# The order of matmuls between attention blocks: projection by halves, product D behind A, the 1x1 convolution behind three taps

## The chip, the core and the metric

The kernel runs on one core of a Trainium2 chip. The time is the device time of one execution, in microseconds (us); several runs are made and their median is compared. A core has a matmul engine (TensorE, PE in the profile, with its weight loads as PEld), a vector engine (VectorE, DVE), an activation engine (ScalarE, ACT), GpSimd (POOL), and SyncE (SP), which issues transfers. Each has its own instruction stream; they meet at semaphores. Matmul results go to PSUM, an accumulator of eight banks of 512 fp32 columns by 128 partitions.

## The reference

Input is x of 8 images, 64 channels, 64 by 64 pixels, fp32. Two layers follow each other.

```
q, k, v = 1x1 projections of x                 # 64 to 64 channels
q, k    = q - mean(q), k - mean(k)             # mean over the pixels
out     = softmax(q^T k / 8) v  +  softmax(mean(q)^T k) v
x2      = x + out
s       = bn(conv1x1(sign(x2))) + bn(conv3x3(sign(x2))) + bn(conv5x5(sign(x2)))
gate    = sigmoid(grouped 16x16 product of mean(s) + gb), channels permuted
result  = s * gate + x2
```

The convolution weights are signs (of the weights less their mean) times a scale for each output channel. So the convolutions are products of numbers like -1, 0 and 1 and can be done in bf16 without loss; the attention stays in fp32.

## The kernel before

Two images lie together on the 128 partitions (64 channels each), which makes four pairs. A pair has 8 query blocks (`NQ`) of 512 pixels, and a block has 32 key tiles (`NK`) of 128 pixels: 32 blocks in all, g = 0 to 31.

**Main loop** (`attend`, line 904). For each key tile j: `scores` (line 461, four matmuls on 64x64 quarters of the array, into one of two score buffers of two banks, pool `ps_s`), an exponential on ACT (line 472, tile `e`, four buffers), then for the tile before it `weighted` (line 480, accumulated in `acc`, the only buffer of pool `ps_a`) and `summed` (line 495, on DVE, which adds up the e tiles). Every instruction is put down in this order by hand (`manual_schedule`); `plan(g)` says what else goes behind which key tile.

**Between blocks.** Behind the first key tile's scores of block g and the last `weighted` of block g-1 come, in this order: `weighted_out` (line 502, ACT copies `acc` to SBUF), in some blocks a small matmul (the gate, the mean scores of the next pair, or the unary part), then `mix_rows` (line 824), then `sums` (line 511, the softmax denominators, tile `su`). `mix_rows` does two things at once on the array: the projection of the queries of block g+1, and the convolutions of block g-3. This happens with both parts in 28 passages between blocks, and once more, without the projection, at the last block. Only the first blocks have a projection alone, and near the end another routine (`mix`) takes over.

**What mix_rows computes.** The projection `q` is split by pixels in two tiles: pq of half 0 has 128 columns, pq of half 1 has 384 (`split_queries`, line 446). Both are fp32[...]. The 5x5 convolution is done for pairs of output rows: `S` (10 products of 256 columns) goes to both rows of a pair, `D` (5 products) to both with opposite signs, `A` and `B` (10 each) to one row each (`row_product`, line 660). The 1x1 is one product of 512 columns and the 3x3 nine (`conv_tap`, line 725). "Half" h means the half of the array's rows (partitions 0 to 63 or 64 to 127) that feeds a product; b, the image, is the half of its columns. Half 0 does q of half 0, S, 1x1 and 3x3; half 1 does q of half 1, D, A and B; each for b = 0 and 1.

**What sets their order.** Each of the four sequences (b, h) gives each of its products a length in units (0.5 for 256 columns of bf16, 1.0 for 512; q is 1.0 in half 0 and 3.0 in half 1) and so a nominal start; all are sorted by it (line 845), and the second key of the sort decides among those with equal starts.

**Where results go.** PSUM tiles of tag "m" (pool `ps_m`, two buffers of one bank) are taken in turn by pq of half 0, pq of half 1, then zD and z1 at their first product, and then by su. z3 uses a bank of the `acc` buffer. S, A and B (tile z5) use a score buffer: S one bank, A and B the halves of the other. The reads are: `split_queries_out` (line 453, DVE, twice), which frees the pq buffers; for D two ACT instructions that start the sum tile `sb` (line 682); adds to `sb` on DVE (line 678) for 1, for S (twice), for A and for B; a copy of z3 by ACT (line 698); and the last add on DVE (line 703). A result whose name is in the test inside the loop ("D1") is read out as soon as its products are in the stream; the others follow behind the loop, in the order of the string there ("3SAB").

Of the kernel before, what the change touches and what calls it, by code (L numbers as in the profile page):

```python
# [44 lines left out]
def conv_seq_kernel(ctx, tc, x, wq, wk, wv, vecs, w1, w3, w5, wtap, gw, out):  # L45
# [16 lines left out]
    def m_tile(name):  # L62
        return ps_m.tile([P, QB], F32, tag="m", name=name)
# [760 lines left out]
    def mix_rows(q, c):  # L824


        seqs = {}
        for b in range(2):
            half0, half1 = [], []
            if q is not None:  # L830
                half0.append(("q", 0, 1.0))
                half1.append(("q", 0, 3.0))
            if c is not None:
                sums = [("S", i, 0.5) for i in range(10)]
                half0 += sums + [("1", 0, 1.0)] + [("3", i, 1.0) for i in range(9)]
                half1 += [("D", i, 0.5) for i in range(5)]
                half1 += [(n, i, 0.5) for n in "AB" for i in range(10)]
            seqs[b, 0], seqs[b, 1] = half0, half1
        order = []
        for (b, h), seq in seqs.items():  # L840
            at = 0.0
            for t in seq:
                order.append((at, b != h, b, h, t))
                at += t[2]
        order.sort(key=lambda o: o[0:2])
        if c is not None:
            p, (r0, _, y, qb) = c
            z, name = {}, f"{p.name}_{qb}"
        if q is not None:
            q[0].query_tiles(q[1])  # L850
        left = {}
        for o in order:
            left[o[4][0]] = left.get(o[4][0], 0) + 1
        for _, _, b, h, (n, i, _) in order:
            if n == "q":
                q[0].split_queries(q[1], b, h)
            else:
                if n not in z:
                    if n in "1D":
                        z[n] = m_tile(f"z{n}_{name}")  # L860
                        if n == "D":
                            z[n] = z[n][:, 0 : QB // 2]
                    elif n == "3":
                        z[n] = acc_banks(f"z3_{name}")[0]
                    elif n in "SAB":
                        t = score_banks(f"z5_{name}")
                        z["S"] = t[0][:, 0 : QB // 2]
                        z["A"], z["B"] = t[1][:, 0 : QB // 2], t[1][:, QB // 2 :]
                if n in "13":
                    p.conv_tap((r0, ROWS, y, qb), {0: [z.get("1")], 1: [z.get("3")]}, b, 0, int(n) // 2, i, i == 0, i == 8 or n == "1")  # L870
                else:
                    p.row_product(z, b, (n, i), r0)
            left[n] -= 1
            if left[n] == 0:
                if n == "q":
                    q[0].split_queries_out(q[1])
                elif n in "D1":
                    p.row_out(qb, z, n)
        if c is not None:
            for n in "3SAB":  # L880
                p.row_out(qb, z, n)
            p.row_end(qb)

# [20 lines left out]
    def attend(pairs):  # L904
# [9 lines left out]
        def plan(g):  # L914
# [26 lines left out]
            def both():  # L941
                q = block(g + 1) if g + 1 < n_blocks else None
                if g == 0:
                    mix(q, None)
                else:
                    mix_rows(q, rows(g - 3) if g >= 3 else None)
# [270 lines left out]
```

## Time and profile before

| | |
|---|---|
| time, median of 3 runs | 1993.19 us (1992.76 to 1994.49) |
| span of the profiled execution | 1993.0 us |
| granted TensorE clock, mean | 0.995 of full speed |
| from one passage's su to the next | 59.87 us, or 60.90 in blocks that also compute the next pair's values |
| key-tile iteration | 1.72 us |
| scores, exponential, weighted: one instruction | 591 ns, 1024 ns, 589 ns |
| 64x256 bf16 product, record | 270 ns |
| L682 (ACT, D), L678 (DVE, 1x1 add), L703 | 1.02 us for two, 0.75, 0.75 us |

In the profile a line such as L660 is a line of the code; "out<-in" names the tiles; the number after x is how many instructions the row joins. The records of the four quarters overlap, so a busy matmul engine may have quarters without work. In the list of waits the first name is who waited and the second who let it go. In the timeline the first column is the start and the second the duration, both in us.

### The profile page before, as it was taken

What the parts mean: (1) busy time and instruction counts of PE and PEld (TensorE: products, weight loads), DVE (VectorE), ACT (ScalarE), POOL (GpSimd) and SP (SyncE); (2) the same over time, 40 slices, a digit from 0 to 9 for tenths busy, and PEclk for the clock granted to TensorE, in tenths of its full rate; (3) what the DMA queues carried; (4) which work ended last, traced back from release to release, by engine and by line L of the source; (5) the groups of instructions that cost most, each with busy time, mean ns of one, the idle gap of its engine ahead of it and who ended that gap; (6) DMA issues with size and microseconds to landing.
All of it is one profiled execution on the core that took longest, in us unless ns stands there. A gap on an engine that the chain in (4) does not pass through costs nothing.

```text
span 1993.0 us, 48278 instructions
## 1 busy us (share of the span) xinstructions
PE 1959.4 (98%) x20946; PEld 777.4 (39%) x20946; DVE 1565.2 (79%) x1739; ACT 1251.8 (63%) x1474; POOL 5.9 (0%) x26
## 2 busy tenths in 40 slices
PE   9999999999999999999999999999999999999997
PEld 4333334343433333343433333333343333333334
DVE  6878877778777798777777778887777778877876
ACT  5666666666666666666666666666666666666663
POOL 0000000000000000000000000000000000000000
PEclk9999999999999999999999999999999999999998
DMA  3010000000001010000001001000000001100001
GB/s 98 9 49 17 14 17 10 15 13 14 17 9 59 17 51 17 15 11 13 15 14 49 19 27 43 14 17 14 13 11 16 14 17 36 32 14 17 17 12 45
DMA packets 43212, 45.84 MB, mean 23 GB/s; under 512 B 15968, under 2 KB 34608, under 8 KB 42864
## 3 DMA queue, kind: packets, MB, share of 16 engines
q1 hardware_dynamic: 42240, 41.49, 7.7%
q8 instruction: 166, 2.72, 0.6%
q10 hardware_dynamic: 720, 1.18, 0.2%
q14 instruction: 54, 0.44, 0.1%
q0 software_dynamic: 32, 0.01, 0.0%
HBM read 14.89 MB, written 8.39 MB: 12 GB/s over the span
## 4 chain that ended last, share of the span: by engine, by line
PE 94%; DVE 4%; ACT 1%; issue 1%; DMA 0%; DVEq 0%; SPq 0%; ACTq 0%
PE ps L461 43%; PE acc L480 42%; PE z L660 2%; DVE es L495 2%; PE z L725 2%; PE pq L446 1%; PE su L511 1%; PE zD L660 1%; PE pv L303 1%; DVE q L453 1%; ACT e L472 0%; DMA x<-in_x 0%; PE warm L149 0%; PE pre L1060 0%; PE po L350 0%
## 5 line engine op out<-in xcount | busy, mean ns | idle before, releaser
L472 ACT ACTIVATE e<-ps 128x1024 f32<-128x1024 f32 x1024 | 1048.9, 1024 | 625.4 <-PE ps L461 589.3
L495 DVE TENSOR_TENSOR es<-es,e 128x1024 f32<-128x1024 f32 x960 | 1170.9, 1220 | 283.4 <-ACT e L472 261.9
L461 PE MATMUL ps<-q,x 64*64 64x512 f32 x8192 | 1067.7, 591 | 0.9 <-DVE kb L159 0.9
L480 PE MATMUL acc<-e,v 64*64 64x512 f32 x8192 | 1063.9, 589 | 0.6 <-ACT e L472 0.3
L480 PEld LDWEIGHTS acc<-e,v 64*64 64x64 f32 x8192 | 310.0, 131 | 570.3 <-ACT e L472 302.6
L461 PEld LDWEIGHTS ps<-q,x 64*64 64x64 f32 x8192 | 307.8, 133 | 543.7 <-issue 286.6
L660 PE MATMUL z<-ec,wc 64*64 64x256 bf16 x580 | 79.4, 272 | 0.0
L678 DVE SCALAR_TENSOR_TENSOR sb<-z,scale,sb 128x256 f32<-128x256 f32 (+1 forms) x87 | 46.9, 566 | 41.1 <-ACT sb L682 41.1
L725 PE MATMUL z<-s,wt 64*64 64x512 bf16 (+2 forms) x694 | 78.6, 367 | 0.5 <-ACT s L591 0.3
L660 PEld LDWEIGHTS <-wc 64*64 64x64 bf16 x1450 | 66.5, 106 | 20.8 <-issue 20.7
L725 PEld LDWEIGHTS <-wt 64*64 64x64 bf16 x860 | 67.5, 107 | 4.6 <-issue 3.0
L524 DVE RECIPROCAL rc<-su 128x128 f32<-128x128 f32 x62 | 58.9, 950 | 0.0
L660 PE MATMUL z<-rs,wc 64*64 64x256 bf16 x435 | 57.8, 270 | 0.0
L682 ACT ACTIVATE sb<-zD,shift,half 128x256 f32<-128x256 f32 x58 | 29.6, 562 | 34.7 <-PE zD L660 34.7
L591 ACT ACTIVATE s<-x,vec 128x512 bf16<-128x512 f32 (+2 forms) x66 | 46.1, 702 | 5.2 <-DVE x L559 5.2
L453 DVE TENSOR_SCALAR q<-pq,mx 128x128 f32<-128x128 f32 (+1 forms) x60 | 26.2, 479 | 29.1 <-PE pq L446 29.1
L493 DVE TENSOR_TENSOR es<-e,e 128x1024 f32<-128x1024 f32 x32 | 39.2, 1224 | 11.1 <-ACT e L472 11.1
L698 ACT COPY r_z<-z 128x512 f32<-128x512 f32 x29 | 17.0, 586 | 37.8 <-PE z L725 37.8
L660 PE MATMUL z<-ec,wt 64*64 64x256 bf16 x290 | 37.9, 274 | 0.0
L660 PE MATMUL z<-rs,wt 64*64 64x256 bf16 x290 | 37.9, 274 | 0.0
L678 DVE SCALAR_TENSOR_TENSOR sb<-z,half,sb 128x256 f32<-128x256 f32 x58 | 25.4, 479 | 12.9 <-PE z L660 12.8
L660 PEld LDWEIGHTS <-wt 64*64 64x64 bf16 x580 | 33.8, 107 | 0.1
(146 smaller groups left out, 686.8 us busy)
## 6 DMA issues: line engine op xcount, KB each, us to landing
r<-rc SPq DMA_DIRECT2D x248, 32.0 KB, 1.9
x<-in_x SPq DMA_DIRECT2D x15, 512.0 KB, 6.1
out<-sb SPq DMA_DIRECT2D x28, 256.0 KB, 2.1
ec<-rs SPq DMA_DIRECT2D x29, 153.0 KB, 2.4
xc<-in_x SPq DMA_DIRECT2D x30, 96.0 KB, 2.5
s<-s SPq DMA_DIRECT2D x31, 66.0 KB, 2.0
y<-y SPq DMA_DIRECT2D x30, 64.0 KB, 2.0
w_tap<-in_wtap SPq DMA_DIRECT2D x2, 560.0 KB, 10.0
```

What stands on the lines that cost most here:

```text
L453: nc.vector.tensor_scalar(q[:, c], self.pq[h][:, 0 : c.stop - c.start], self.mx, None, ALU.subtract)
L461: nc.tensor.matmul(ps[img[h], b, :], self.x[img[b], bass.ds(j * P + h * H, H)], self.q[qb][img[b], :], start=True, stop=neg is None,)
L472: nc.scalar.activation(e, ps, AF.Exp, scale=1.0 / 8.0)
L480: nc.tensor.matmul(self.acc[qb][img[b], h, :], self.v[img[h], j, img[b]], e[img[h], b, :], start=(j == 0), stop=(j == NK - 1),)
L493: nc.vector.tensor_tensor(self.es[qb], self.first, e, ALU.add)
L495: nc.vector.tensor_tensor(self.es[qb], self.es[qb], e, ALU.add)
L524: nc.vector.reciprocal(self.rc[:, c], self.sums_p[:, c])
L591: nc.scalar.activation(sy[n][0][:, rows, pad : pad + HH], self.x2[qb][:, r0 * HH : r1 * HH].rearrange("p (h w) -> p h w", w=HH), AF.Sign, ...
L660: nc.tensor.matmul(z[name][img[b], :].rearrange("p (h w) -> p h w", w=HH), taps[k][img[h], c * C : c * C + C], rows, start=(i == 0), stop= ...
L678: nc.vector.scalar_tensor_tensor(out, data, scale, out, ALU.mult, ALU.add, **kw)
L682: nc.scalar.activation(sv[:, :, t, :], z["D"].rearrange("p (j w) -> p j w", w=HH), AF.Identity, bias=shift, scale=half5[:, t : t + 1],)
L725: nc.tensor.matmul(z[n][h][img[b], 0 : nr * HH].rearrange("p (h w) -> p h w", w=HH), wt[img[h], FIRST[n] + i, :], data, start=first, stop= ...
```

## The change

The order of work inside `mix_rows` is rearranged. (1) Among products with equal nominal start, those of half 0 come first for both images, where before the diagonal quarters came first; so the two short projection matmuls stand ahead of the two long ones. (2) In half 1, D comes behind A, not ahead of it. (3) In half 0, the 1x1 comes behind three taps of the 3x3. (4) The 1x1 result is no longer read within the loop but behind it, and its add stands behind those of S, A and B. The purpose is that products that need a buffer which the projection holds come later than those that don't, and that the add which frees the score buffer comes ahead of those which free less. The products, their number and sizes stay as they are.

```diff
             if c is not None:
                 sums = [("S", i, 0.5) for i in range(10)]
-                half0 += sums + [("1", 0, 1.0)] + [("3", i, 1.0) for i in range(9)]
-                half1 += [("D", i, 0.5) for i in range(5)]
-                half1 += [(n, i, 0.5) for n in "AB" for i in range(10)]
+                taps3 = [("3", i, 1.0) for i in range(9)]
+                half0 += sums + taps3[0:3] + [("1", 0, 1.0)] + taps3[3:]
+                for n, k in (("A", 10), ("D", 5), ("B", 10)):
+                    half1 += [(n, i, 0.5) for i in range(k)]
             seqs[b, 0], seqs[b, 1] = half0, half1
         order = []
         for (b, h), seq in seqs.items():
             at = 0.0
             for t in seq:
-                order.append((at, b != h, b, h, t))
+                order.append((at, h, b, h, t))
                 at += t[2]
         order.sort(key=lambda o: o[0:2])
...
-                elif n in "D1":
+                elif n == "D":
                     p.row_out(qb, z, n)
         if c is not None:
-            for n in "3SAB":
+            for n in "3SAB1":
                 p.row_out(qb, z, n)
             p.row_end(qb)
```

## The prediction

> **What bounds the kernel now.** I read the page first (busy shares and the chain that ended last), then the list of waits, then the timeline of one passage between two blocks. TensorE is the bound everywhere:
>
> ```profile
> PE 1959.4 (98%) x20946; PEld 777.4 (39%) x20946; DVE 1565.2 (79%) x1739; ACT 1251.8 (63%) x1474; POOL 5.9 (0%) x26
> PE 94%; DVE 4%; ACT 1%; issue 1%; DMA 0%; DVEq 0%; SPq 0%; ACTq 0%
> ```
>
> The first line is busy time, the second the chain by engine. The 4% of VectorE in the chain says that the matmul engine is at times held by it, and a busy 98% doesn't say that all four 64x64 quarters of the array work. The list of waits names the places the change can touch (us in total, times, longest):
>
> ```profile
> DVE sb L678 <- ACT sb L682: 41.1, 29, 2.3
> ACT sb L682 <- PE zD L660: 34.7, 28, 2.5
> DVE q L453 <- PE pq L446: 29.1, 30, 1.0
> PE zD L660 <- DVE q L453: 12.5, 28, 0.5
> PEld ps L461 <- DVE sb L678: 7.7, 28, 0.3
> ```
>
> Only the last two are waits of the matmul engine, the others are idle time of engines with room. The one of zD comes 28 times, once in each passage that has a projection and a convolution. A passage between 316 and 323 us:
>
> ```profile
> 316.46 0.27 PE L446 MATMUL pq<-x,mm 64*64 64x128 f32 x1
> 316.68 0.27 PE L660 MATMUL z<-rs,wc 64*64 64x256 bf16 x1
> 316.77 1.01 ACT L502 COPY o<-acc 128x1024 f32<-128x1024 f32 x1
> 316.79 0.48 PE L446 MATMUL pq<-xc,mm 64*64 64x384 f32 x1
> 317.12 0.27 PE L660 MATMUL z<-rs,wc 64*64 64x256 bf16 x1
> 317.41 0.88 DVE L453 TENSOR_SCALAR q<-pq,mx 128x128 f32<-128x128 f32 x2 [1.00 <-PE pq L446]
> 317.81 0.27 PE L660 MATMUL zD<-rs,wc 64*64 64x256 bf16 x1 [0.42 <-DVE q L453]
> 318.59 1.02 ACT L682 ACTIVATE sb<-zD,shift,half 128x256 f32<-128x256 f32 x2 [0.82 <-PE zD L660]
> 320.77 0.64 PE L511 MATMUL su<-es,ones 128*32 128x256 f32 x8
> 320.81 0.87 DVE L678 SCALAR_TENSOR_TENSOR sb<-z,half,sb 128x256 f32<-128x256 f32 x2 [0.42 <-PE z L660]
> 321.61 0.86 DVE L678 SCALAR_TENSOR_TENSOR sb<-z,scale,sb 128x256 f32<-128x256 f32 x2
> ```
>
> The columns are start, duration, instruction, and in brackets the idle time before it. The passage is from the projection's start (316.46) to the sums of the next block (su, 320.77): 4.31 us. In it, zD needs one of two PSUM buffers (tag "m") that both hold the projection pq. It gets one when the first L453 has read it, and that starts only at 317.41, since the last write of the first pq is the fourth matmul in program order, behind both long ones (second passes at 316.79). The S products stop at 317.12, so nothing streams from about 317.23 (317.12 plus one 0.11 step) to 317.81: 0.58 us, of which the trace counts 0.42, since a matmul's record runs on 0.16 past its stream (0.27 less 0.11).
>
> **What the Trainium skill says.** "TensorE: Matmul & The Clock Gate", Part 3 (The mechanism): matmuls in different tiles of the array overlap, but start and end in strict program order. The overlap agrees: four quarters advance one 64x256 product each per 0.11 us. The strict order does not: the S product at 316.68 starts ahead of the projection's second pass at 316.79, which belongs to an earlier instruction. I follow the trace and keep the page's order as a rival. "TensorEngine Tiling (Array Packing)", Gotcha 1: different row tiles may not use one PSUM bank at the same time. The new order keeps to it (S and A lie in two banks, and D, 1 and 3 have their own), so it costs nothing; no trace shows a collision. "Perfetto Trace Analysis", Optimization Strategy: find the gaps of the most contended engine and what blocks it; that is the zD wait.
>
> **The change part by part.**
>
> *Projection of half 0 first.* The four matmuls are the same, now in the order h0, h0, h1, h1. The first pq is complete after two short ones, at about +0.37 from the start (0.22 of streaming, 0.16 of tail), not +0.95. The first L453 (0.36) can then end by about +0.8, the second (0.5) by +1.5, instead of +1.31 and +1.83. Neighbours in the same row half are no loss: half steps of half 1 already issue two such in a row at 0.11 a step.
>
> *D behind A.* What follows the projection in half 1 is ten A products, which need no "m" buffer but a bank of the score buffer that S already has. zD is first needed at 0.66 (384 columns in two passes: +0.34 plus 0.32) plus ten steps of 0.11, +1.76. Its buffer is free by +0.8, at worst +1.35. The wait of zD goes.
>
> *1x1 behind three taps.* z1 needs the second pq buffer; it now comes at 0.22 + 10 x 0.11 + 3 x 0.22 = +1.98, after its release at +1.5 (at worst +1.87). In its place 3x3 comes first, at 0.22 + 1.10 = +1.32. That needs the accumulator bank, which L502 releases at 317.78, +1.32, plus 0.04 as between L453 and zD: a wait of some 0.04 us takes over. Bounds: 0 and 0.1 (if the restart of the quarters costs as much again).
>
> *Length without stalls.* Half 0 sets it: 0.22 + 0.01 + ten S at 0.11 + ten 512-column taps at 0.22 + 0.09 of tail before su = 3.62. The last convolution of the kernel, with no projection, is a check from the trace: its first z starts at 1899.82, su at 1903.27, 3.45, against my 3.62 - 0.22 = 3.40. With the 0.04: 3.66.
>
> *A new wait of su.* su reuses the buffer of zD, which ACT must have read twice (L682, 1.02). D ends at 0.66 + 15 x 0.11 + 0.04 = +2.35, its record at +2.51; ACT from +2.55 to +3.57; su from +3.61. That is 0.05 ahead of when su would start anyway: just hidden, and behind su on TensorE stands everything. Bounds: nothing, or 0.1 if half 1 lags a step. The S adds wait for the same ACT pair and for the end of the products (+3.7), so they start as before relative to su.
>
> *Adds: S, A, B ahead of 1 and 3.* S, S, A, B still take 1.7 us after su and release the score bank that the third score block (323.11) needs, its weights at 322.68: 0.17 us of room now (322.47 plus 0.04), unchanged. The 1x1 add (0.75, at 319.64 now, in idle time) moves behind them. VectorE is then 0.75 later with the first es add; in the steady loop it idles 0.49 an iteration, so it has caught up after two. In the three blocks that also store (716 to 743 us) it is saturated, but the matmuls keep their 1.72 an iteration there, and it idled 1.7 us earlier in that block. At the two passages after them the mean's matmul waits behind its queue; I allow 1 us in all, between 0 and 2.
>
> *Sum.* 19 regular passages: 4.31 - 3.66 = 0.65, so 12.4. Nine carry a small matmul first (mean, unary or gate; 3 each), whose result blocks the second pq; from there to su is 4.35 (683.83 to 688.18). There half 0 runs ahead, half 1 needs 0.66 + 25 x 0.11 + 0.09 = 3.50, and su waits for ACT until 3.57: 0.78 each, 7.0. Less 1.0: 18.4. 1993.2 - 18.4 = 1974.8, about 1975.
>
> **The rivals.** *Only what the trace counts comes back:* 12.5 us, 1980.7; with strict program order S would start at +0.34 and not +0.22, 28 x 0.12 = 3.4 off the gain, 1978. Together some 1980. For it: the page, and new waits within 0.1 of biting. Against: the S start. *Waits swap places:* 3x3 on L502, su on L682 and the bank release each lose 0.2, and the time stays near 1993. For it: three margins of 0.05 to 0.17. Against: each is a difference of measured times, and not all add. *Slower:* if D ends only with the whole mix, su stands behind 1.02 of ACT plus 0.08; 1.10 - 0.65 = +0.45 a passage, 28 times: 2006. For it: D is later than before, and su has everything behind it. Against: ten B products (1.1 us) follow D in half 1.
>
> **How the numbers follow.** Forecast 0.69, half-way case 0.16, swap 0.06, slower 0.09. One passage (502 to 507 us) runs at a granted clock of 0.66; its coming or going is worth some 2 us, and the new-wait bounds (28 x 0.1 = 2.8) come on top: 1971 below. Above, the half-way case and its spread: 1982. Faster takes the first two, 0.85; same 0.06; slower 0.09.
>
> **What would show it.** zD's wait for L453 gone from the list; 3x3's first tap behind L502 by under 0.1; su behind L682 by under 0.1; the passage near 3.66; L703 0.75 later after su. I am wrong if su names L682 with some tenths, if S starts later than +0.22, or if the score weights slip behind L678.

## The result and the profile after

The changed kernel takes 1974.8 us (median of 4 runs, 1973.93 to 1977.97), the kernel before in the same comparison 1993.84 us (4 runs, 1992.76 to 1994.88). The ratio is 0.9907, with a 95% interval of 0.989 to 0.9925: about 19 us faster. The prediction was 1975.0, between 1971 and 1982.

The page of the profile after shows the same two lines as were shown of before, busy time and the chain that ended last:

```profile
PE 1951.9 (99%) x20946; PEld 776.0 (39%) x20946; DVE 1565.9 (79%) x1739; ACT 1250.8 (63%) x1474; POOL 5.9 (0%) x26
PE 92%; DVE 3%; DMA 3%; ACT 2%; issue 1%; DVEq 0%; SPq 0%; ACTq 0%
```

TensorE has the same 20946 matmuls and is as good as always busy, before and after; the page alone would not tell that anything was gained. The 3% of DMA is nearly all (2.1%) put down to 18 loads of `xc`, the pixels of a later projection, of 2.3 us each. ACT's second read of zD waits for several semaphores, one of them that of such a load, and the load lands about when this read starts. But this read starts 0.46 us after the first read in the kernel after and also in the version "D inside A" below, whose chain has 0% of DMA; so the load holds nothing up. The start of the program varies: the first su lay at 80.89 and 78.71 us in two profiles of the unchanged kernel. So from here on two measures leave the start out: the length of a passage between blocks, from the projection's first matmul to su, and the time from the third su to the last, which holds 27 of the 28 passages with a projection and the last one without. That time is 1704.10 us before and 1686.58 after, 17.5 less of the 19.7 us between the two spans; of the rest, 2.1 lie ahead of the third su.

The list of waits answers the one of before. zD's wait for L453 (12.5 us, 28 times) is no longer in it, and L453 now idles 15.9 us and not 29.1 for the projection. One wait of a TensorE queue is new, the weights of su behind L682:

```profile
ACT sb L682 <- PE zD L660: 49.5, 29, 2.9
DVE q L453 <- PE pq L446: 15.9, 33, 0.7
PEld su L511 <- ACT sb L682: 9.8, 29, 0.4
```

A passage in the timeline of after (start, duration, instruction, idle time before it), the one that stood between 316 and 323 us before:

```profile
313.68 0.27 PE L446 MATMUL pq<-x,mm 64*64 64x128 f32 x1
313.90 0.27 PE L660 MATMUL z<-rs,wc 64*64 64x256 bf16 x1
313.99 1.01 ACT L502 COPY o<-acc 128x1024 f32<-128x1024 f32 x1
314.01 0.48 PE L446 MATMUL pq<-xc,mm 64*64 64x384 f32 x1
314.14 1.05 DVE L453 TENSOR_SCALAR q<-pq,mx 128x128 f32<-128x128 f32 x2 [0.51 <-PE pq L446]
...
315.05 0.40 PE L725 MATMUL z<-s,wt 64*64 64x512 bf16 x2
...
315.53 0.27 PE L660 MATMUL zD<-ec,wc 64*64 64x256 bf16 x1
...
315.92 0.41 PE L725 MATMUL z<-s,wt 64*64 64x512 bf16 x2
315.98 0.27 PE L660 MATMUL zD<-rs,wc 64*64 64x256 bf16 x1
...
316.38 1.02 ACT L682 ACTIVATE sb<-zD,shift,half 128x256 f32<-128x256 f32 x2 [1.38 <-PE zD L660]
...
317.45 0.16 PEld L511 LDWEIGHTS su<-es,ones 128*32 128x32 f32 x8 [0.36 <-ACT sb L682]
317.45 0.64 PE L511 MATMUL su<-es,ones 128*32 128x256 f32 x8
317.60 0.88 DVE L678 SCALAR_TENSOR_TENSOR sb<-z,half,sb 128x256 f32<-128x256 f32 x2 [2.40 <-PE z L725]
318.39 1.65 DVE L678 SCALAR_TENSOR_TENSOR sb<-z,scale,sb 128x256 f32<-128x256 f32 x3
```

Each fp32 matmul of the projection stands in the trace as two records, its two passes (240 records for 120 matmuls): 313.68 is a first pass, 314.01 a second one. The passage is 317.45 less 313.68, 3.77 us, where it was 4.31. L453 starts 0.46 after the passage's start and not 0.95, zD starts without a wait, the first tap of the 3x3 comes 0.05 after L502 has ended (313.99 + 1.01 = 315.00). At its end su waits: L682 ends at 317.40 and su starts at 317.45.

The whole gain, by passages, in us each:

| | before | after | times | gain |
|---|---|---|---|---|
| plain passage | 4.31 | 3.77 | 19 | 10.3 |
| with the mean scores first | 4.73 | 4.03 | 3 | 2.1 |
| with the unary part first | 6.54 | 4.23 | 1 | 0.7, and 1.6 of clock |
| the same, at full clock | 4.93 | 4.23 | 2 | 1.4 |
| with the gate first | 5.45 | 4.75 | 3 | 2.1 |
| the last, without a projection (from its first S to su) | 3.45 | 3.66 | 1 | -0.2 |
| the first two, with a projection alone | 1.97, 1.91 | 1.38, 1.31 | 2 | 1.2 |

The sum is 19.2, for 19.0 between the medians. In the first two passages su needs the buffer that L453's first read gives back, and before it waited 0.52 us for it in each; now that read is done in time. The clock entry is the passage from 502 us on, which ran at a low granted clock before. Its block took 64.44 us where its two like took 62.83; after, all three take 62.13. That is 0.70 less for the two and 2.3 less for the one, 1.6 beyond the 0.70. The stretches of before, then of after, around this passage (stretch; length, busy time of PE, PEld, DVE, ACT, POOL; granted clock; DMA):

```profile
500.00:502.00 2.00, 1.79 (x22) 1.25 (x23) 0.39 (x2) 1.14 (x5) 0.00 (x0) 1.00 0.00 0
502.00:504.00 2.00, 1.56 (x30) 1.56 (x33) 0.87 (x2) 0.25 (x1) 0.00 (x0) 0.59 0.17 49
504.00:506.00 2.00, 2.00 (x37) 2.00 (x33) 0.75 (x1) 0.77 (x2) 0.00 (x0) 0.55 0.09 25
```

```profile
496.00:498.00 2.00, 1.85 (x44) 1.59 (x47) 1.14 (x4) 0.72 (x5) 0.00 (x0) 1.00 0.00 0
498.00:500.00 2.00, 2.00 (x60) 2.00 (x54) 0.20 (x1) 0.79 (x2) 0.00 (x0) 1.00 0.26 73
```

PE is busy in both; it is the column ahead of the DMA's, the clock, that falls to 0.59 and 0.55 in one and stays at 1.00 in the other. Taken over 502.4 to 505.8 us alone it is 0.50. The profile of the kernel after has such a stretch too, at another place: 0.51 from 79.1 to 82.5 us. It cost about as much: from the first su to the second there are 59.19 us, against 57.49 in the version "D inside A", which has the same two first passages and the full clock there.

### The profile page after: what moved, and what is told of

It is laid out like the page before. It is cut to its first block, busy times and chain, and to the rows that moved or that the text cites. A ratio compares the mean times of both kernels' runs of the same rounds, so it can differ in the third digit from the quotient of the medians.

```text
span 1973.3 us, 48307 instructions
## 1 busy us (share of the span) xinstructions
PE 1951.9 (99%) x20946; PEld 776.0 (39%) x20946; DVE 1565.9 (79%) x1739; ACT 1250.8 (63%) x1474; POOL 5.9 (0%) x26
## 4 chain that ended last, share of the span: by engine, by line
PE 92%; DVE 3%; DMA 3%; ACT 2%; issue 1%; DVEq 0%; SPq 0%; ACTq 0%
PE ps L461 43%; PE acc L480 43%; DVE es L495 2%; DMA xc<-in_x 2%; PE z L660 1%; PE su L511 1%; PE z L725 1%; PE pq L446 1%; PE pv L303 1%; ACT e L472 1%; ACT sb L682 1%; DMA x<-in_x 0%; ACT o L502 0%; PE warm L149 0%; PE po L350 0%
## 5 line engine op out<-in xcount | busy, mean ns | idle before, releaser
L660 PEld LDWEIGHTS <-wc 64*64 64x64 bf16 x1450 | 78.8, 105 | 1.1 <-issue 0.6
L660 PE MATMUL z<-ec,wc 64*64 64x256 bf16 x580 | 73.7, 270 | 0.0
L682 ACT ACTIVATE sb<-zD,shift,half 128x256 f32<-128x256 f32 x58 | 29.6, 560 | 49.5 <-PE zD L660 49.5
L725 PEld LDWEIGHTS <-wt 64*64 64x64 bf16 x860 | 46.1, 105 | 5.8 <-issue 3.3
L453 DVE TENSOR_SCALAR q<-pq,mx 128x128 f32<-128x128 f32 (+1 forms) x60 | 29.0, 484 | 17.4 <-PE pq L446 15.9
L502 ACT COPY o<-acc 128x1024 f32<-128x1024 f32 (+2 forms) x33 | 32.3, 982 | 1.2 <-PE acc L480 1.2
L446 PE MATMUL pq<-xc,mm 64*64 64x128 f32 (+1 forms) x120 | 29.3, 385 | 2.7 <-ACT gt L764 2.0
```

What stands on the lines that cost most here:

```text
L446: nc.tensor.matmul(self.pq[h][img[b], 0:w], mm[img[h], img[h]], data, start=True, stop=True)
L660: nc.tensor.matmul(z[name][img[b], :].rearrange("p (h w) -> p h w", w=HH), taps[k][img[h], c * C : c * C + C], rows, start=(i == 0), stop= ...
L682: nc.scalar.activation(sv[:, :, t, :], z["D"].rearrange("p (j w) -> p j w", w=HH), AF.Identity, bias=shift, scale=half5[:, t : t + 1],)
L725: nc.tensor.matmul(z[n][h][img[b], 0 : nr * HH].rearrange("p (h w) -> p h w", w=HH), wt[img[h], FIRST[n] + i, :], data, start=first, stop= ...
```

## The experiments

The theory from the prediction: what counts is when the first pq is complete and who asks for its buffer; each part of the change then has a place in that chain. The rivals: the sort alone would do it; D's place alone would do it; the 1x1's place matters, or doesn't; the order of the adds is for nothing; and a late D costs more than it brings. Each ratio is to the kernel before on the same chip in the same comparison (1994.65 us in the first four, 1993.02 in the next four, 1992.53 in the last two). Most of the intervals overlap with that of the change (0.989 to 0.9925); where they do, what is said below of a difference rests on the traces. "Special" passages are those with mean scores, unary part or gate first.

| kernel | median, us | ratio, 95% interval | plain passage | third su to last |
|---|---|---|---|---|
| sort alone | 1977.78 | 0.9922 (0.9904 to 0.994) | 3.86 | 1690.33 |
| change with the old sort | 1974.53 | 0.9896 (0.988 to 0.9913) | 3.74 | 1686.18 |
| change with the 1x1 add ahead of S | 1984.65 | 0.9946 (0.993 to 0.9963) | 3.77 | 1696.25 |
| old sort, 1x1 ahead of the 3x3 | 1976.72 | 0.9906 (0.989 to 0.9923) | 3.75 | 1687.19 |
| D inside A | 1973.02 | 0.9904 (0.9888 to 0.9921) | 3.66 | 1684.04 |
| D last | 2007.21 | 1.0075 (1.0058 to 1.0092) | 4.89 | 1718.13 |
| D inside A, 1x1 add in the loop | 1971.82 | 0.9895 (0.9879 to 0.9912) | 3.66 | 1684.06 |
| before once more | 1994.3 | 1.0006 (0.9997 to 1.0015) | 4.31 | 1704.16 |
| half 1 first behind the projection | 1971.81 | 0.9892 (0.9875 to 0.9908) | 3.66 | 1684.71 |
| 1x1 first, D behind eight A | 1971.75 | 0.9889 (0.9873 to 0.9906) | 3.61 | 1683.23 |

**The sort alone**, the kernel before with only the projection's order changed:

```diff
-                order.append((at, b != h, b, h, t))
+                order.append((at, h, b, h, t))
```

> The kernel before with the sort key alone changed (half 0 first among equal starts). My theory (zD waits because the first pq counts as written only when the fourth matmul in program order is done): the first read of pq ends near +0.82 us from the start of the projection, zD wants its buffer at +0.66 and waits about 0.2 instead of 0.58, z1 at +1.32 then waits for the second read, ending near +1.5. Passage about 3.85 us against 4.31, nine passages with a small matmul 0.6 shorter; time about 1980. Rival (the move of D behind A is what brings the gain, the sort nothing): within 4 us of before, 1990 or more.

Measured: 1977.78, a plain passage of 3.86, the special ones 0.44 shorter than before (0.6 were expected). zD starts 0.86 after the passage's start:

```profile
311.76 0.27 PE L446 MATMUL pq<-x,mm 64*64 64x128 f32 x1
...
312.62 0.27 PE L660 MATMUL zD<-ec,wc 64*64 64x256 bf16 x1
...
313.32 0.40 PE L725 MATMUL z<-y,wt 64*64 64x512 bf16 x2
```

The long projection matmuls have streamed at +0.66, so zD still stands some 0.2 behind L453's first read, but S goes on meanwhile and the list counts no wait. This one line takes 13.8 us (1704.10 less 1690.33) of the 17.5; 1.6 of either are the clock's. What it also leaves is that z1, first of the 512-column products, waits for the second pq buffer (L453 ends its second read at 313.27, z1 starts at 313.32).

**The change with the old sort**, so without the line above:

```diff
-                order.append((at, h, b, h, t))
+                order.append((at, b != h, b, h, t))
```

> The changed kernel with the old sort key: D behind A, 1x1 behind three taps, 1x1 add last, but the projection in its old order. My theory: zD is then needed at +1.76 and its buffer is free at +1.35 also with the old projection, z1 at +1.98 against +1.87, so nothing waits: as the changed kernel, 1975 within 2 us. Rival (the order of the projection is needed as well): z1 or zD still wait some tenths, 1980 or more.

Measured: 1974.53 and 3.74, a shade shorter than the whole change. The two parts are two ways to the same half microsecond: the sort lets the first buffer go earlier, D behind A asks for it later. With D behind A the sort is not needed in these passages. In the first two, with a projection alone, it is: they take 1.97 and 1.90 here, as before, and 1.38 and 1.31 in every version with the new sort.

**The 1x1 add ahead of S**, all else as in the change:

```diff
-            for n in "3SAB1":
+            for n in "31SAB":
```

> The changed kernel with the 1x1 add ahead of the S, A and B adds. My theory: the add waits for ACT's start of sb, which with D this late ends only as the passage ends, so the score bank comes free 0.75 us later, which eats the 0.17 us of room and costs about 0.6 to 0.7 us in each of 29 passages: about 1994. Rival (the order of the adds lies off the path, VectorE has room): 1975 within 1.5 us.

Measured: 1984.65, 9.7 us in the time from the third su to the last, so 0.35 a passage. It isn't in the passage (3.77) but behind it. The timeline of this experiment:

```profile
317.92 0.75 DVE L678 SCALAR_TENSOR_TENSOR sb<-z,scale,sb 128x512 f32<-128x512 f32 x1 [2.24 <-PE z L725]
317.94 0.64 PE L511 MATMUL su<-es,ones 128*32 128x256 f32 x8
319.57 0.87 DVE L678 SCALAR_TENSOR_TENSOR sb<-z,scale,sb 128x256 f32<-128x256 f32 x2
320.56 0.24 PEld L461 LDWEIGHTS ps<-q,x 64*64 64x64 f32 x8 [0.98 <-PE ps L461]
320.59 1.09 PE L461 MATMUL ps<-q,x 64*64 64x512 f32 x8
```

The add of the 1x1 (0.75) stands ahead of the adds of S, A and B, which free the score bank at 320.44 (319.57 + 0.87), 2.50 after su, and the score block follows at 320.59, 2.65 after su. In the kernel after, the add of B ends at 319.26, 1.81 after su, and the score block starts at 319.79, 2.34 after it. The order of the adds is thus needed while D stands behind all ten A, for then VectorE can't do the 1x1 ahead of su any more (with D behind three A it can, as shown below). The size was smaller than expected. I had put the room at 0.17, from the weights' start; but released weights and matmul lie only 0.03 apart (320.56 and 320.59), where in the kernel after they lie 0.42 apart (319.37 and 319.79). As an estimate from these figures, the room is 0.75 less what was lost, 0.35: about 0.4.

**Old sort and the 1x1 ahead of the 3x3**, the case in which I expected z1 to wait for the second pq:

```diff
-                half0 += sums + taps3[0:3] + [("1", 0, 1.0)] + taps3[3:]
+                half0 += sums + [("1", 0, 1.0)] + taps3
...
-                order.append((at, h, b, h, t))
+                order.append((at, b != h, b, h, t))
```

> Old sort, D behind A, 1x1 add last, but the 1x1 product ahead of the 3x3 taps as before. My theory: the wait moves from zD to z1, which is needed at +1.32 and gets its buffer at +1.87, so the quarters stall about 0.5 us and the passage is near 4.2 us: about 1990, with a wait of z1 for L453 of 0.4 to 0.5 us in each passage. Rival (moving D is enough): 1976 or less, no such wait.

Measured: 1976.72 and 3.75; the expectation failed. The timeline tells why:

```profile
314.75 0.27 PE L446 MATMUL pq<-x,mm 64*64 64x128 f32 x1
315.70 0.87 DVE L453 TENSOR_SCALAR q<-pq,mx 128x128 f32<-128x128 f32 x2 [1.00 <-PE pq L446]
316.10 0.37 PE L725 MATMUL z<-y,wt 64*64 64x512 bf16 x1
316.63 0.27 PE L660 MATMUL zD<-rs,wc 64*64 64x256 bf16 x1
```

z1 starts 1.35 after the passage's start, when only the first read of L453 is over (the second ends at 316.57), and zD comes second, right behind that second read. Buffers go to whoever asks first, and with D behind A that is z1. "z1 needs the second pq buffer" was true only while zD stood ahead of it. So with D behind ten A and the old sort, the place of the 1x1 is worth 0.01 in a plain passage. In the special ones it is worth 0.12 (4.16, 4.36 and 4.88 here, 4.04, 4.24 and 4.76 in the change with the old sort), and in the last it costs 0.2: 1.0 us in all (1687.19 less 1686.18).

**D inside A**, behind three of its products, the rest as in the change:

```diff
-                for n, k in (("A", 10), ("D", 5), ("B", 10)):
-                    half1 += [(n, i, 0.5) for i in range(k)]
+                abd = [[(n, i, 0.5) for i in range(k)] for n, k in (("A", 10), ("D", 5), ("B", 10))]
+                half1 += abd[0][0:3] + abd[1] + abd[0][3:] + abd[2]
```

> The changed kernel with the five D products behind three of the ten A products instead of behind all ten. My theory: in the 19 plain passages of the changed kernel su starts 0.11 us late because it waits for ACT's second read of zD; with D 0.77 us earlier that wait is gone and they shorten from 3.77 to about 3.66 us, the nine others stay: 19 x 0.11 = 2.1, about 1973. Rival (su is held by the end of the products, the ACT wait only coincides): as the changed kernel, 1975 within 1 us, passage 3.77.

Measured: 3.66 in plain passages, and su's wait for L682 is gone from the list. 3.66 is the length that the prediction gave for a passage without stalls and with the 0.04 of L502, so the 0.11 between that and the change's 3.77 is su's wait for D. The special passages gain 0.07 as well (3.96 for 4.03), which I had not expected: su had stood behind L682 there too.

**D last**, behind B, to see the side of the prediction that said slower:

```diff
-                for n, k in (("A", 10), ("D", 5), ("B", 10)):
+                for n, k in (("A", 10), ("B", 10), ("D", 5)):
```

> The changed kernel with D last in half 1 (A, B, D). My theory: su then stands behind two ACT reads that start only when the passage's products end, so the passage grows by about 0.95 us to 4.7: 28 times, about 2002, slower than before, and su waits for L682 about 1 us each time. Rival (ACT's reads are hidden whatever the place of D): 1975 within 2 us.

Measured: 2007.21, slower than before, a plain passage of 4.89. The list of waits and the timeline of this experiment:

```profile
PE su L511 <- ACT sb L682: 32.9, 29, 1.2
```

```profile
318.76 0.27 PE L660 MATMUL zD<-rs,wc 64*64 64x256 bf16 x1
...
319.17 1.02 ACT L682 ACTIVATE sb<-zD,shift,half 128x256 f32<-128x256 f32 x2 [2.50 <-PE zD L660]
...
320.24 0.64 PE L511 MATMUL su<-es,ones 128*32 128x256 f32 x8 [1.15 <-ACT sb L682]
```

su waits behind both reads of ACT with nothing else on TensorE, 1.15 us in this passage and 32.9 us in 29. The mechanism of the "slower" rival is real; the change escapes it only because ten B products follow D.

**D inside A, with the 1x1 added in the loop again**, to price VectorE's lateness, which the prediction held to be 1 us:

```diff
-                elif n == "D":
+                elif n in "D1":
...
-            for n in "3SAB1":
+            for n in "3SAB":
```

> The kernel with D behind three A products, and besides the 1x1 add read within the loop, ahead of the S adds, as before. My theory: with D early ACT has started sb by about +2.9, so the 1x1 add runs in VectorE's idle time ahead of su and costs nothing; and the 0.75 us that it put VectorE back in the next block costs nothing either: same as with D behind three A products, within 1 us. Rival (VectorE's late start costs in the saturated blocks): 1 to 2 us faster than that one. Third way (the add ends just after su and delays the score bank): slower by 3 us or more.

Measured: 1684.06 from the third su to the last, against 1684.04 with the late add. VectorE's lateness costs nothing that the traces show; the medians differ by 1.2 us, which their overlapping intervals don't tell from no difference.

**The kernel before once more**, to see which of its traits recur:

> The kernel before, again, for a second profile. If the passage of 64.4 us with a clock of 0.66 around 505 us belongs to the program, it is there again; if it is chance, that passage takes about 62.8 us as its two like (at 995 and 1483 us), and the span is about 1.6 us shorter. The first us of the program (to the first su at 80.9 us) may differ by 1 to 2 us either way, since it hangs on transfers. Time 1993 to 1994.

Measured: 1994.3, and again 64.47 us in the block with the low clock, and 4.31, 4.73, 6.57 and 5.45 in the passages. So the low clock in that one passage stands in both profiles of the kernel before and in none of the ten of changed kernels. But four of these ten have a stretch of 3.4 us at half clock that neither profile of the kernel before has, from 78 or 79 us on: the change, the old sort with the 1x1 first, D last, and D inside A with the 1x1 add in the loop. How often either comes in runs without a profile isn't known. The mean clock differs between runs of one kernel: of the 15 runs of the kernel before that the second four are compared with, four had 0.997 or 0.998 and took 1990.76 to 1991.82 us, the others 0.995 or 0.996 and 1992.55 to 1994.91.

**Half 1 first behind the projection**, to see why L682 starts 0.13 after D's record in the kernel after and not 0.04:

```diff
-                order.append((at, h, b, h, t))
+                order.append((at, h if t[0] == "q" else 1 - h, b, h, t))
```

> The changed kernel, with half 1 instead of half 0 first among equal starts for all products but the projection, so that the last D product stands ahead of the 3x3 tap of the same nominal start. My theory: in the changed kernel ACT's first read of zD starts 0.13 us behind the record of the last D product in a plain passage, and not 0.04, because the completion of a matmul counts only once those ahead of it in program order are done, and the 512-column tap ahead of it runs on 0.08 longer. With the order turned the read starts within 0.06 of D's record, su 0.08 earlier, passage 3.69: about 1.5 us in all. Rival (the delay has another cause, the order of the streams doesn't matter): 0.13 again, passage 3.77.

Measured: 3.66. In program order D's last products now stand ahead of the 3x3 tap that streams beside them, and in the timeline ACT starts 0.04 after D's record (314.62 + 0.27 = 314.89), which is also the median of all 29 passages:

```profile
314.62 0.27 PE L660 MATMUL zD<-rs,wc 64*64 64x256 bf16 x1
314.63 0.41 PE L725 MATMUL z<-s,wt 64*64 64x512 bf16 x2
...
314.93 1.02 ACT L682 ACTIVATE sb<-zD,shift,half 128x256 f32<-128x256 f32 x2 [1.22 <-PE zD L660]
```

In the kernel after, that tap (315.92, 0.41 long) is ahead in program order and ends at 316.33. D's records end at 316.25, but ACT starts at 316.38, 0.05 after the tap (0.13 after D's record is again the median of 29). So the end of D's product was told only when the tap ahead of it in program order had ended. Besides, D's last product starts 0.07 earlier in the passage with the order turned (+2.23 for +2.30). Both together are more than su's delay of 0.11, so it no longer waits and the passage has the length of D inside A.

**The 1x1 first and D behind eight A**, a version built from the above: z1 takes the first pq's buffer, D comes a little earlier, and the 3x3 comes after L502 without a wait:

```diff
-                half0 += sums + taps3[0:3] + [("1", 0, 1.0)] + taps3[3:]
-                for n, k in (("A", 10), ("D", 5), ("B", 10)):
-                    half1 += [(n, i, 0.5) for i in range(k)]
+                half0 += sums + [("1", 0, 1.0)] + taps3
+                abd = [[(n, i, 0.5) for i in range(k)] for n, k in (("A", 10), ("D", 5), ("B", 10))]
+                half1 += abd[0][0:8] + abd[1] + abd[0][8:] + abd[2]
```

> The changed kernel with the 1x1 ahead of the 3x3 taps and D behind eight of the ten A products. My theory: z1, the first to ask, gets the buffer of the first pq, free at +0.82, so at +1.32 it waits for nothing; the 3x3 comes at +1.54, behind the release of acc at +1.36, so its wait (and the restart of the quarters) goes as well; zD at +1.54 gets the second buffer, free at +1.51, and ends early enough for su. Passage 3.60 to 3.63 instead of 3.77, the last one 3.45 instead of 3.66: 1970.5 to 1971.5. Rival (with D behind three A products everything was won, 3.66 is the length of the work): 3.66 in a plain passage, 1972.

Measured: 1971.75 (1969.64 to 1971.89) and 3.61, against 3.62 for a passage without any stall; the last passage is back at 3.45. By the traces it is 3.4 us shorter than the change from the third su to the last. Its ratio of 0.9889 can't be told from that of the other three versions in which ACT has read D in time, nor, by the intervals, from that of the change.

## Why the prediction was right

**zD's wait goes: right.** S starts at +0.22 from the passage's start, L453's second read ends at +1.51 (predicted +1.5), zD asks at +1.85 and waits for nothing. That S starts at 313.90, ahead of the second pass of the long projection matmul at 314.01, again differs from what the Trainium skill says in "TensorE: Matmul & The Clock Gate", Part 3 (The mechanism), that matmuls start in program order; the rival that rested on it (1978 to 1980) falls. On ends the trace agrees with the page: ACT starts 0.13 after D's record in the kernel after, against 0.04 with half 1 first.

**3x3 behind L502: right.** Its first tap starts at +1.37; 1.32 + 0.04 were predicted.

**su just hidden behind L682: the step that failed, by a tenth.** I had ACT reading D from +2.55 to +3.57, 0.05 ahead of su. It read from +2.70 to +3.72: D's record ends 0.06 later than worked out, and the tap ahead of it in program order adds 0.09. So su waits, and a plain passage is 3.77, not 3.66: 0.54 gained and not 0.65, 2.1 us in 19. The upper bound that I had given, 0.1, was about what happened. With D inside A, or half 1 first, ACT is done in time and the passage is 3.66. The same wait made the special passages 0.70 shorter instead of 0.78, 0.7 in nine.

**VectorE's lateness: too dear.** L703 starts 2.69 after su and not 1.81, later by 0.88 where 0.75 was expected, but it costs 0 and not 1.0, by the pair of experiments with D inside A.

**The clock: in the range, not in the sum.** Between the two profiles the low clock of one passage went, and 1.6 us with it. In "TensorE: Matmul & The Clock Gate", Part 1 (What's actually happening), the Trainium skill says that the clock halves when the array was idle for a window of about 3.4 us. The 0.50 over 3.4 us agrees with half. No such idle time shows here, though: ahead of it PE is busy 1.79 us of the stretch from 500 to 502, in part with matmuls of a single column (lines 350 and 353), and 1.39 of the last 2.00, in which zD's wait lies. The 0.58 us without streaming, which the change takes away, would be a cause near at hand, but it isn't shown: the stretch from 79.1 us in the kernel after came without it, behind the same single-column matmuls and with PE busy 1.85 of the 2.00 us ahead, and D inside A, with the same 1.85 from 76 to 78 us, had none. Why it comes stays open, and with it whether the 1.6 us are the change's.

**The last passage** has no projection, and my sum had no term for it. There D behind A gains nothing, and the 3x3, now first, waits for L502: 0.2 lost. With the 1x1 first it is not (3.45).

**The first two passages**, with a projection alone, had no term either: 0.6 gained in each, 1.2, from the sort.

The terms then are 18.4 - 2.1 - 0.7 - 0.2 + 1.0 + 1.6 + 1.2 = 19.2, as in the table. The mechanism and its largest terms were right, but that 18.4 came so near to the 19.0 of the medians is in part luck: 3.0 us too much in the sum stand against 3.8 that it had no term for or took off for nothing.

**The rivals.** The swap of waits did come about for su, at 0.11 and not with the 0.2 it needed in each place. The room of the score bank, one of its three margins, was about 0.4 and not 0.17. The slower case needed D at the end of the mix, where it is 2007 against the 2006 worked out.

Two of the change's parts bring little once D is behind A: the sort, 1.2 us in the first two passages, and the 1x1 behind three taps, 1.0 with the old sort. The order of the adds is worth 9.7 with D behind ten A, and nothing with D behind three.

## What to carry to other kernels

When several products share few PSUM buffers, write down for each who asks in program order, when the buffer is read out, and what stands behind it: moving the asker later and the reader earlier are two ways to one gain, and doing both brings little more. A product whose read stands before the end of the stretch has both a first and a last good place; here behind three A products and, with the 1x1 first, behind eight were both good, and behind ten was a tenth of a microsecond too late. In the pair of versions that tried it here, a product's end counted only when a longer one ahead of it in program order had ended too, so put a short product that others wait for ahead of a long one that starts beside it.

## What the hardware showed that was not expected

- Matmuls in other quarters of the array start ahead of an earlier instruction's second pass (313.90 against 314.01), but D's end was told in program order: ACT started 0.13 us after D's record with a longer tap ahead, 0.04 with the tap behind.
- Weights and matmul of a score block lay 0.42 us apart where weights had come early, and 0.03 apart where they were released late (320.56 and 320.59). The start of a weight load is no measure of the room.
- The granted clock fell to half for 3.4 us at a time, with TensorE busy for 1.32 (old sort, 1x1 first) to 1.85 (the kernel after) of the 2.00 us ahead, and cost 1.6 to 1.7 us each: from 502 us on in both profiles of the kernel before, from 78 or 79 us on in four of ten profiles of changed kernels.
